# Cross-attention and a state-space scan on one core: the denominators' products placed later, features in contiguous chunks, and a planner with longer transfer times

## The chip, the core and the metric

The kernel runs on one core of one Trainium2 chip. Its engines are TensorE (PE in the profile, its weight loads PEld), VectorE (DVE), ScalarE (ACT), GpSimd (POOL) and SyncE (SP), which here does nothing but issue DMAs. The metric is the device time of one execution in microseconds (us). All data is float32.

## The reference

With T = 4096 rows of x, 3202 rows of context, a width H = 512, 8 heads of 64 and a state of 64, the reference computes (batch 1):

```python
xq  = layernorm(x, g1, beta1);  kv = layernorm(ctx, g1, beta1)
q, k, v = xq @ Wq.T + bq, kv @ Wk.T + bk, kv @ Wv.T + bv      # 8 heads of 64
x1  = x + softmax(q k.T / 8) v @ Wo.T + bo                     # over all 3202 keys
u   = (layernorm(x1, g2, beta2) @ W_in.T + b_in) @ Bmat        # [4096, 64]
s_t = silu(s_{t-1} @ A.T) + u_t                                # scan over 4096 steps
out = x1 + s @ Cmat + mean(ctxb) @ W_prog.T + b_prog
```

The token ids have no part in the output.

## The kernel before

**Stages.** For the first 215 us or so the kernel normalizes the context in 26 chunks of 128 rows, turns each (TensorE transposes, L285), and makes keys (pk) and values (pv), which it stores in DRAM in the layout in which they will be read. Small pieces of work (biases, the folded weight of the state's input, the first queries) are threaded between the chunks (`side`). Then comes the attention, and from about 1945 us on the end of the scan and the output.

**Attention.** The queries are cut into 8 blocks Q of 512 rows, each into 4 pairs of heads hp and 2 halves of 256 rows: 64 units. A unit goes through the keys in 13 steps of up to 256 keys. In a step, TensorE makes the scores s (L649: 16 matmul instructions of 64x64 by 64x256, four of which lie beside each other in the array), ACT takes their exponential p (L719), VectorE, or GpSimd at steps 2, 6 and 10, adds p to the unit's running sum acc (L727), and four steps later TensorE multiplies p with the values into po (L759). A maximum over sampled keys (sm, L667 and L686) gives the shift of the exponent. At the end of a unit the sum is folded on GpSimd (`fold`, L734), and `sums` multiplies it with ones on TensorE: pd (L777, 8 matmul instructions), the denominators. ACT reads pd (L811), VectorE adds its two parts (L815), takes the reciprocal (L818), scales the unit's output (L825) and reduces once for a check (L821).

**Around a block.** When the units of a half are done, the output projection pa multiplies with Wo (L1000), VectorE adds the residual rows (x1, L1013), which GpSimd has prepared (xr, L994), and the rows are normalized, turned and multiplied into the scan's input (pu, L1056). Queries of the next block are loaded, normalized, turned and multiplied (pq, L318). In the middle blocks (0 < Q < 7) rows are not turned by TensorE: VectorE transposes squares of 32x32 (`flip`, L946), and `move` (L951) puts the squares in their places by DMA, 16 DMAs of 32 KB for each pair of tiles, four in each of four pieces of the plan.

**Features.** The 512 features of a row lie on 128 partitions in 4 chunks. For queries and for the rows after the first sum, before has feature 4p + c in chunk c of partition p (`slice(c, None, NC)` in `transposes`), so a partition's features are contiguous in the weight's rows and a move goes in pieces of 256 floats. The weight of the queries, its gain and its bias (raw_q, g1q, be1q) and those of the second norm (g2s, be2s) are loaded in that order, the gains and biases by 16 small DMAs. The context's features are in contiguous chunks of 128.

**The order of work.** The program is written by hand for the first stage. For the rest, `Plan` (L68) orders pieces of work: each has an engine, an estimated cost in ns, a due time, pieces after which it comes, and rings of buffers that it takes and that other pieces give back. `Plan.order` runs a clock over them: an engine that is free takes the ready piece that is due first; what depends on a piece on another engine becomes ready `LATE` ns after it ends (L76; for SP this stands for the time of a transfer). A step is due every STEP = 2150 ns. The order so found is the order of instructions on each engine; on the chip engines wait for each other by semaphores, and each engine's instructions run in this order. The ring `m` has two PSUM banks, used in turn by pd (both), pa (both), pq, pu and the transposes (tp). `from_(d)` (L847) names the score step that belongs to a due time, so that a piece can be held behind it. K and V tiles are loaded 10 and 6 steps ahead, from the same SP queue as moves, rows (xr) and queries (x).

The pieces that the change touches are `sums` in `finish` (L800) and the `move` pieces in `queries` (L882) and `project` (L978):

```python
plan.add(("sums", i), "PE", 450, partial(sums, w), [("fold", i)], d + 1000,
         ["s"] if last else ["m", "m"], [("acc", ("add", i, 1))], "quarters")
...
plan.add((*ks[0], f"move{a}"), "SP", 1300, partial(move_, a), ...
```

Here d is the time of a unit's last product, and `last` is true for the last unit alone.

In the last unit pd is called pd_last and takes a bank pair of the ring s; the products of the last half's outputs with Wo are called yb (L1347), and are in the plan as pieces ("last", c), the last of which need the last unit's scaled output.

Of the kernel before, what the change touches and what calls it, by code (L numbers as in the profile page):

```python
# [20 lines left out]
P = 128  # L21
TB = 32
# [45 lines left out]
class Plan:  # L68
# [6 lines left out]

    LATE = {"PE": 110, "DVE": 130, "ACT": 110, "POOL": 100, "SP": 3000}  # L76
    ENTER, LEAVE = 110, 147
# [93 lines left out]
def xattn_ssm_kernel(  # L171
# [50 lines left out]
    be2s = const.tile([P, NC], F32, name="be2s")  # L222
    g1q = const.tile([P, NC], F32, name="g1q")
    be1q = const.tile([P, NC], F32, name="be1q")
    bqkv = const.tile([P, 3 * NC], F32, name="bqkv")
# [78 lines left out]
    def turned(xn, xh, t, name):  # L304

        tp = transposes(None, "m", xh, P, name)
        yield
        n = 2 * TB
        nc.scalar.copy(
            xn[:, t * P // n : (t + 1) * P // n].rearrange("p a c k -> p c a k"),  # L310
            tp.rearrange("p c (a k) -> p c a k", k=n),
        )
# [21 lines left out]
    def first_queries(x0):  # L334

        xn = first_xn["xn"] = xnp.tile([P, QB // (2 * TB), NC, 2 * TB], F32, tag="xn", name="xn_0")
# [12 lines left out]
        pieces = heads(0, 0, xn)  # L349
        next(pieces)  # L350
        for _ in pieces:
            yield
        yield
# [14 lines left out]
    def fetch_w(k, queue, part=slice(0, NC)):  # L368
        of = wsrc if k else wqkv_t.rearrange("(p c) o -> p c o", c=NC)
        queue.dma_start(raw[k][:, part], of[:, part, k * H : (k + 1) * H])  # L370

    def gain(k, w):
        for i in range(NC):
            nc.vector.tensor_scalar(
                w[:, i, :], raw[k][:, i, :], (g1s if k else g1q)[:, i : i + 1], None, ALU.mult
            )
# [9 lines left out]
    def shift(k):  # L386

        t = weighted(raw[k], be1s if k else be1q, f"shift_{k}")
# [14 lines left out]
        yield  # L403


    def side():
# [43 lines left out]
        for i in range(NC):  # L450
            nc.tensor.matmul(
                pt[:, i, :NS], wct[:, i::NC], twice, start=True, stop=True
            )
# [64 lines left out]

    def turned_c(xh, n, name):
        return transposes(kps, "t", xh, n, name, lambda c: slice(c * P, (c + 1) * P))  # L520

    def turn_chunk(c):
        if c < NCH:
            g, n = c // GC, keys(c)
            if c % GC == 0:
                cts[g] = ctp.tile([P, NC, GC * CK], F32, tag="ct", name=f"ct_{g}")
            o = key0(c) - key0(g * GC)
            copy = nc.vector.tensor_copy if c % 2 else nc.scalar.copy
            copy(cts[g][:, :, o : o + n], turned_c(xhs.pop(c), n, f"c{c}"))  # L529

    with tc.manual_schedule():
# [7 lines left out]
        load_chunk(3)  # L539
        for t, src in ((be1s, beta1), (bqkv, b_qkv)):  # L540
            nc.sync.dma_start(t, src)
        for c in range(4, 7):
            load_chunk(c)
        for t, src in ((g1q, g1), (be1q, beta1), (g2s, g2), (be2s, beta2)):
            for k in range(NC):
                n = P // NC
                nc.sync.dma_start(t[k * n : (k + 1) * n], src.rearrange("(p c) k -> k p c", c=NC)[k])
        norm_chunk(0)
# [251 lines left out]
    def finish(w, i, d, plan):  # L800
# [22 lines left out]
        def scale(part):  # L823
# [58 lines left out]
    def queries(plan, Q, d):  # L882
# [3 lines left out]
        for half in range(2):  # L886
# [17 lines left out]
            def open_(half=half):  # L904
                if half == 0:
                    w["xn"] = xnp.tile([P, QB // (2 * TB), NC, 2 * TB], F32, tag="xn", name=f"xn_{Q}")

            def move_(a, half=half, v=v, open_=open_):
                if a == 0:
                    open_()  # L910
                move(w["xn"][:, half * P // TB : (half + 1) * P // TB], v["x"], a)

            def turn(half=half, nv=nv, at=at, v=v, open_=open_):
                open_()
                xn = w["xn"][:, half * P // TB : (half + 1) * P // TB]
# [6 lines left out]
            if mixes(Q):  # L922
# [21 lines left out]
    def flip(pair, xh, t):  # L944

        nc.vector.transpose(  # L946
            pair.rearrange("p t h -> p (t h)").rearrange("p (b c t r) -> p t b c r", b=P // TB, c=NC, t=2)[:, t],
            xh.rearrange("p (b r c) -> p b c r", b=P // TB, c=NC),
        )

    def move(xn, pair, a):  # L951

        of = pair[a * TB : (a + 1) * TB].rearrange("p t h -> p (t h)").rearrange(
            "p (b c k) -> p b c k", b=P // TB, c=NC
        )
        for b in range(P // TB):
            nc.sync.dma_start(xn[b * TB : (b + 1) * TB, a], of[:, b])

# [19 lines left out]
    def project(plan, Q, halves, d, index):  # L978

        for half in halves:  # L980
# [71 lines left out]
            def inputs(w=w, at=at, last=last):  # L1052
                w["pu"] = m_tile([P, P], f"pu_{at[0]}")
                for c in range(NC):
                    for t in range(2):
                        nc.tensor.matmul(  # L1056
                            w["pu"][t * NS : (t + 1) * NS], wc[:, c, :],
                            w["xn"][:, t, c, :] if last else w["xn"][:, :, c, t * TB : (t + 1) * TB],
                            start=(c == 0), stop=(c == NC - 1), skip_group_check=True,
                        )  # L1060
# [20 lines left out]
            else:  # L1081
                copied, xn2, after = [], (*ks[0], "move0"), 16

                def move_(a, w=w, at=at):
                    if a == 0:
                        w["xn"] = xp_.tile([P, P // TB, NC, 2 * TB], F32, tag="xn2", name=f"xn2_{at[0]}", bufs=1)
                    move(w["xn"], w["x1"], a)
# [5 lines left out]
                for a in range(P // TB):  # L1093
                    plan.add((*ks[0], f"move{a}"), "SP", 1300, partial(move_, a),
                             [(*k, "flip") for k in ks] + ([xn2] if a else []), d + (6 + 2 * a) * STEP,
# [256 lines left out]
    def last_rows(plan, d):  # L1352
# [26 lines left out]
        def turn_(g):  # L1379
            if g:  # L1380
                tp = v["tp"][g] = sv["pyl"].rearrange("p (c k) -> p c k", c=NC)
                for c in range(NC):
                    nc.tensor.transpose(tp[:, c, :], v["xh"][g][:, c::NC], ident)
            else:
# [269 lines left out]
    def attend():  # L1654
# [31 lines left out]
        def turned_():  # L1686
# [6 lines left out]
            for c in range(NC):  # L1693
                nc.tensor.transpose(banks[0][:, c * P : (c + 1) * P], xh[:, c::NC], ident)
            nc.scalar.copy(xn, banks[0].rearrange("p (c k) -> p c k", c=NC))
# [204 lines left out]
```

## Time and profile before

| | us |
|---|---|
| median of 3 runs | 2019.77 |
| lowest and highest | 2015.93, 2020.21 |
| the profiled execution | 2018.0 |
| its span, first to last instruction | 2016.0 |
| TensorE busy | 1965.9 (98%) |
| VectorE busy | 1277.6 (63%) |
| ScalarE busy | 1131.9 (56%) |
| GpSimd busy | 791.7 (39%) |
| DMA queue of SP, share of 16 engines | 32.5% |
| granted TensorE clock, mean | 0.991 |

The profile is of one execution. A group is named by its line, engine and operation and by the tiles that it writes and reads (out<-in). Matmul instructions are pipelined: one is counted as busy until its modelled end, so groups overlap in the list, and the starts tell the rate at which they issue. Lines of the view in order of time have start, length, engine, line, operation, tiles, shape and count, and in brackets the idle time of the engine before it and what ended it. Lines of the view of waits have the waiting group, what ended the wait, and the total in us, the times and the longest. Lines of the table by stretches have the stretch, its length, the busy us (and instructions) of PE, PEld, DVE, ACT and POOL, the granted TensorE clock as a share of full speed, the DMA engines' share and GB/s.

### The profile page before, as it was taken

The page shows a single profiled execution, that of the slowest core. Times are in us where ns is not written, and L with a number is a line of the kernel's source. Part 1 is how long each engine was busy: PE and PEld are TensorE (multiplying, and loading weights), DVE is VectorE, ACT ScalarE, POOL GpSimd, SP SyncE. Part 2 cuts the span into 40 slices and gives each one's busy share as a digit, 9 for nine tenths or more (in the row PEclk, how much of TensorE's full clock was granted, in tenths as well). Part 3 has the DMA queues.
Part 4 walks back from the last instruction along what each step waited for, and adds up shares of the span by engine and source line. Part 5 has one row for each costly group of instructions (what it writes and reads, how often), then busy time and mean ns, then how long its engine had stood idle before and what let it go on. Part 6 is the DMA issues. An engine that isn't in the chain of part 4 may idle for free.

```text
span 2016.0 us, 66547 instructions
## 1 busy us (share of the span) xinstructions
PE 1965.9 (98%) x29070; PEld 1261.4 (63%) x29070; DVE 1277.6 (63%) x1533; ACT 1131.9 (56%) x1478; POOL 791.7 (39%) x631
## 2 busy tenths in 40 slices
PE   8999999999999999999999999999999999999996
PEld 4444566666566666666666666666666666666774
DVE  4221367566866687567856686668756665666585
ACT  2233466565556556655656656655665665655653
POOL 2111244344533444345424443344434552444424
PEclk9999999999999999999999999999999999999998
DMA  5632323223322233223322332223312321445476
GB/s 170 190 99 66 102 82 98 65 81 104 103 76 78 88 102 98 61 74 98 96 62 80 105 103 77 78 86 103 98 57 78 98 75 59 139 132 154 135 200 200
DMA packets 209014, 204.29 MB, mean 101 GB/s; under 512 B 29576, under 2 KB 182152, under 8 KB 208716
## 3 DMA queue, kind: packets, MB, share of 16 engines
q1 hardware_dynamic: 204168, 192.28, 32.5%
q10 hardware_dynamic: 4548, 7.67, 1.2%
q8 instruction: 231, 3.78, 0.8%
q14 instruction: 67, 0.55, 0.1%
HBM read 156.33 MB, written 29.88 MB: 92 GB/s over the span
## 4 chain that ended last, share of the span: by engine, by line
PE 91%; DVE 3%; POOL 2%; issue 1%; DMA 1%; ACT 1%; SPq 0%; DVEq 0%; ACTq 0%; POOLq 0%
PE po L759 33%; PE s L649 33%; PE pq L318 6%; PE pa L1000 5%; PE pk L598 4%; PE pv L565 4%; PE pd L777 2%; DVE acc L727 1%; PE pu L1056 1%; PE sm L667 1%; PE po L747 1%; ACT p L719 1%; POOL acc L734 1%; PE tp_c L285 1%; DMA xr<-in_x_dram 0%
## 5 line engine op out<-in xcount | busy, mean ns | idle before, releaser
L719 ACT ACTIVATE p<-s,shifts 128x1024 f32<-128x1024 f32 (+1 forms) x832 | 886.7, 1080 | 557.5 <-PE s L649 539.8
L649 PE MATMUL s<-q,k 64*64 64x256 f32 x12800 | 841.1, 379 | 3.5 <-ACT p L719 2.5
L759 PE MATMUL po<-p,v 64*64 64x256 f32 x12800 | 834.1, 378 | 0.4 <-DVE o L798 0.4
L727 DVE TENSOR_TENSOR acc<-p,acc 128x1024 f32<-128x1024 f32 (+1 forms) x515 | 625.4, 1214 | 319.1 <-POOL acc L727 270.2
L727 POOL TENSOR_TENSOR acc<-p,acc 128x1024 f32<-128x1024 f32 x189 | 460.7, 2437 | 706.0 <-DVE acc L727 380.0
L649 PEld LDWEIGHTS s<-q,k 64*64 64x64 f32 x12800 | 490.9, 133 | 229.2 <-ACT p L719 24.6
L759 PEld LDWEIGHTS po<-p,v 64*64 64x64 f32 x12800 | 494.5, 134 | 198.4 <-issue 12.3
L734 POOL TENSOR_TENSOR acc<-acc 128x512 f32<-128x512 f32 x64 | 89.7, 1401 | 116.4 <-DVE acc L727 114.2
L727 DVE TENSOR_TENSOR acc<-p,p 128x1024 f32<-128x1024 f32 x64 | 100.6, 1572 | 48.4 <-ACT p L719 42.8
L318 PE MATMUL pq<-xn,wq 128*128 128x512 f32 x256 | 118.3, 605 | 0.0
L818 DVE RECIPROCAL rd<-rd 128x256 f32<-128x256 f32 (+1 forms) x65 | 112.3, 1728 | 2.2
L1000 PE MATMUL pa<-wo,o 128*128 128x512 f32 x240 | 107.0, 599 | 0.0
L713 DVE TENSOR_TENSOR acc<-x,acc 2x256 f32<-2x256 f32 x128 | 97.6, 762 | 2.9
L565 PE MATMUL pv<-wv,ct 128*128 128x512 f32 (+1 forms) x208 | 96.3, 616 | 1.0 <-ACT ct L529 0.7
L598 PE MATMUL pk<-ct,wk 128*128 128x512 f32 (+1 forms) x224 | 88.8, 549 | 0.0
L318 PEld LDWEIGHTS pq<-xn,wq 128*128 128x128 f32 x256 | 46.0, 189 | 57.6 <-issue 56.3
L1000 PEld LDWEIGHTS pa<-wo,o 128*128 128x128 f32 x240 | 44.4, 190 | 56.0 <-issue 55.8
L327 ACT ACTIVATE q<-pq,bias 128x512 f32<-128x512 f32 x32 | 22.0, 687 | 98.6 <-PE pq L318 98.6
L529 DVE COPY ct<-tp_c 128x512 f32<-128x512 f32 (+1 forms) x13 | 8.5, 651 | 105.7 <-PE tp_c L285 105.7
L798 DVE TENSOR_TENSOR o<-po,o 128x256 f32<-128x256 f32 x64 | 27.0, 421 | 71.2 <-ACT o L794 70.8
L994 POOL TENSOR_TENSOR xr<-xr,rowb 128x512 f32<-128x512 f32 x30 | 45.9, 1544 | 57.6 <-DMA xr<-in_x_dram 57.6
L565 PEld LDWEIGHTS pv<-wv,ct 128*128 128x128 f32 (+1 forms) x208 | 38.3, 193 | 44.8 <-issue 42.6
(215 smaller groups left out, 1221.2 us busy)
## 6 DMA issues: line engine op xcount, KB each, us to landing
k<-kd SPq DMA_DIRECT2D x432, 128.0 KB, 2.2
v<-vd SPq DMA_DIRECT2D x432, 128.0 KB, 2.2
xn<-x SPq DMA_DIRECT2D x416, 32.0 KB, 1.9
xr<-in_x_dram SPq DMA_DIRECT2D x30, 256.0 KB, 3.7
x1d<-xr SPq DMA_DIRECT2D x30, 256.0 KB, 2.7
x<-in_x_dram SPq DMA_DIRECT2D x28, 256.0 KB, 3.5
cx<-in_ctx_dram SPq DMA_DIRECT2D x25, 256.0 KB, 3.2
vd<-vs SPq DMA_DIRECT2D x25, 256.0 KB, 2.2
```

The costliest lines, as they stand in the source:

```text
L318: nc.tensor.matmul(pq, wq[:, i, hp * P : (hp + 1) * P], xn[:, :, i, :], start=(i == 0), stop=(i == NC - 1),)
L565: nc.tensor.matmul(pv[h * HD : h * HD + n, :H], ct[:, k, o : o + n], wv[:, k, :], start=(i == 0), stop=(i == NC // parts - 1), skip_group_ ...
L598: nc.tensor.matmul(pk[:, :n_g], wk[:, i, hp * P : (hp + 1) * P], ct[:, i, :n_g], start=(i == 0), stop=(i == NC - 1),)
L649: nc.tensor.matmul(s[k0 : k0 + HD, a, b, :], kts[(*w["at"][:2], c)][r, b * CK + k0 : b * CK + k0 + HD], q[r], start=True, stop=True, skip_ ...
L713: nc.vector.tensor_tensor(to[r], t[r], to[r], ALU.add)
L719: nc.scalar.activation(t[:, :, :nb, :], w["ps"][c][:, :, :nb, :], AF.Exp, bias=w["shift"])
L727: engine.tensor_tensor(w["acc"][:, :, :nb, :], t[:, :, :nb, :], before[:, :, :nb, :], ALU.add)
L734: nc.gpsimd.tensor_tensor(acc[:, :, 0, :], acc[:, :, 0, :], acc[:, :, 1, :], ALU.add)
L759: nc.tensor.matmul(w["po"][a * HD : (a + 1) * HD, k, :QU], vts[Q, hp, c][r, b, a * HD : (a + 1) * HD], t[r, a, b, :], start=(c == 0 and b ...
L818: nc.vector.reciprocal(w["rd"][:, part], w["rd"][:, part])
L994: nc.gpsimd.tensor_tensor(v["x"], v["x"], rowb, ALU.add)
L1000: nc.tensor.matmul(v["pa"], o_t[Q, c, half][:, t * P : (t + 1) * P], wo[:, c, :], start=(c == 0), stop=(c == NC - 1),)
```

## The change

There are four parts.

1. `sums` of all units but the last is held behind the score step that is due six steps after the unit's last product.
2. Queries and rows have their features in contiguous chunks of 128 like the context: `transposes` takes columns c*128 to (c+1)*128, `xn` is [128, 4, rows] instead of [128, rows/64, 4, 64], the query weight is read like the others, and the separate gains and biases (g1q, be1q) and the 16 small loads go; g2s and be2s come by one DMA each. `flip` reads its squares contiguously.
3. `move` issues as many DMAs of the same size, each in pieces of 64 floats (256 bytes) instead of 256 floats.
4. In the plan a piece of four moves costs 2600 instead of 1300, and `LATE` of SP is 5000 instead of 3000.

```diff
-    LATE = {"PE": 110, "DVE": 130, "ACT": 110, "POOL": 100, "SP": 3000}
+    LATE = {"PE": 110, "DVE": 130, "ACT": 110, "POOL": 100, "SP": 5000}
...
-    def transposes(pool, tag, xh, n, name, of=lambda c: slice(c, None, NC)):
+    def transposes(pool, tag, xh, n, name):
...
-                tp[:, c, :n], xh[:n, of(c)], ident[:n, :n]
+                tp[:, c, :n], xh[:n, c * P : (c + 1) * P], ident[:n, :n]
...
-                xn[:, :, i, :],
+                xn[:, i, :],
...
-        of = wsrc if k else wqkv_t.rearrange("(p c) o -> p c o", c=NC)
-        queue.dma_start(raw[k][:, part], of[:, part, k * H : (k + 1) * H])
+        queue.dma_start(raw[k][:, part], wsrc[:, part, k * H : (k + 1) * H])
...
-        for t, src in ((be1s, beta1), (bqkv, b_qkv)):
+        for t, src in ((be1s, beta1), (bqkv, b_qkv), (g2s, g2), (be2s, beta2)):
             nc.sync.dma_start(t, src)
         for c in range(4, 7):
             load_chunk(c)
-        for t, src in ((g1q, g1), (be1q, beta1), (g2s, g2), (be2s, beta2)):
-            for k in range(NC):
-                n = P // NC
-                nc.sync.dma_start(t[k * n : (k + 1) * n], src.rearrange("(p c) k -> k p c", c=NC)[k])
...
-        plan.add(("sums", i), "PE", 450, partial(sums, w), [("fold", i)], d + 1000,
+        plan.add(("sums", i), "PE", 450, partial(sums, w),
+                 [("fold", i)] + ([] if last else [from_(d + 6 * STEP)]), d + 1000,
                  ["s"] if last else ["m", "m"], [("acc", ("add", i, 1))], "quarters")
...
-                    plan.add((*ks[0], f"move{a}"), "SP", 1300, partial(move_, a),
+                    plan.add((*ks[0], f"move{a}"), "SP", 2600, partial(move_, a),
...
     def flip(pair, xh, t):
 
         nc.vector.transpose(
-            pair.rearrange("p t h -> p (t h)").rearrange("p (b c t r) -> p t b c r", b=P // TB, c=NC, t=2)[:, t],
-            xh.rearrange("p (b r c) -> p b c r", b=P // TB, c=NC),
+            pair.rearrange("p t h -> p (t h)").rearrange("p (g t r) -> p t g r", t=2, r=TB)[:, t],
+            xh.rearrange("p (g r) -> p g r", r=TB),
         )
 
     def move(xn, pair, a):
 
+        n = 2 * TB
         of = pair[a * TB : (a + 1) * TB].rearrange("p t h -> p (t h)").rearrange(
-            "p (b c k) -> p b c k", b=P // TB, c=NC
+            "p (c b k) -> p b c k", b=P // TB, k=n
         )
         for b in range(P // TB):
-            nc.sync.dma_start(xn[b * TB : (b + 1) * TB, a], of[:, b])
+            nc.sync.dma_start(xn[b * TB : (b + 1) * TB, :, a * n : (a + 1) * n], of[:, b])
...
-                            w["xn"][:, t, c, :] if last else w["xn"][:, :, c, t * TB : (t + 1) * TB],
+                            w["xn"][:, t, c, :] if last else mixed(w["xn"][:, c, :], t),
```

The same change of columns and shapes is made in `turned`, `first_queries`, `side`, `open_`, the rows of the last half and the slow path that runs only if a check of the softmax or the scan fails.

More of the change, by code (lines that the diff above doesn't have):

```diff
@@ L222, in xattn_ssm_kernel @@
     be2s = const.tile([P, NC], F32, name="be2s")
-    g1q = const.tile([P, NC], F32, name="g1q")
-    be1q = const.tile([P, NC], F32, name="be1q")
     bqkv = const.tile([P, 3 * NC], F32, name="bqkv")
@@ L307, in turned @@
         yield
[L308 to L312, printed above, removed]
+        nc.scalar.copy(xn[:, :, t * P : (t + 1) * P], tp)
     def heads(Q, hp, xn):
@@ L334, in first_queries @@
     def first_queries(x0):
-        xn = first_xn["xn"] = xnp.tile([P, QB // (2 * TB), NC, 2 * TB], F32, tag="xn", name="xn_0")
+        xn = first_xn["xn"] = xnp.tile([P, NC, QB], F32, tag="xn", name="xn_0")
         for t in range(NT):
@@ L374, in gain @@
             nc.vector.tensor_scalar(
-                w[:, i, :], raw[k][:, i, :], (g1s if k else g1q)[:, i : i + 1], None, ALU.mult
+                w[:, i, :], raw[k][:, i, :], g1s[:, i : i + 1], None, ALU.mult
             )
@@ L386, in shift @@
     def shift(k):
-        t = weighted(raw[k], be1s if k else be1q, f"shift_{k}")
+        t = weighted(raw[k], be1s, f"shift_{k}")
         yield
@@ L451, in side @@
             nc.tensor.matmul(
-                pt[:, i, :NS], wct[:, i::NC], twice, start=True, stop=True
+                pt[:, i, :NS], wct[:, i * P : (i + 1) * P], twice, start=True, stop=True
             )
@@ L517, in norm_chunk @@
             xhs[c] = normalize(cxs.pop(c), keys(c), f"c{c}", pool=cin)
-    def turned_c(xh, n, name):
-        return transposes(kps, "t", xh, n, name, lambda c: slice(c * P, (c + 1) * P))
     def turn_chunk(c):
@@ L528, in turn_chunk @@
             copy = nc.vector.tensor_copy if c % 2 else nc.scalar.copy
-            copy(cts[g][:, :, o : o + n], turned_c(xhs.pop(c), n, f"c{c}"))
+            copy(cts[g][:, :, o : o + n], transposes(kps, "t", xhs.pop(c), n, f"c{c}"))
     with tc.manual_schedule():
@@ L905, in open_ @@
                 if half == 0:
-                    w["xn"] = xnp.tile([P, QB // (2 * TB), NC, 2 * TB], F32, tag="xn", name=f"xn_{Q}")
+                    w["xn"] = xnp.tile([P, NC, QB], F32, tag="xn", name=f"xn_{Q}")
             def move_(a, half=half, v=v, open_=open_):
@@ L910, in move_ @@
                     open_()
-                move(w["xn"][:, half * P // TB : (half + 1) * P // TB], v["x"], a)
+                move(w["xn"][:, :, half * QU : (half + 1) * QU], v["x"], a)
             def turn(half=half, nv=nv, at=at, v=v, open_=open_):
                 open_()
-                xn = w["xn"][:, half * P // TB : (half + 1) * P // TB]
+                xn = w["xn"][:, :, half * QU : (half + 1) * QU]
                 v["turns"] = [turned(xn, nv[t]["xh"], t, f"x{at[t]}") for t in range(2)]
@@ L1085, in move_ @@
                     if a == 0:
-                        w["xn"] = xp_.tile([P, P // TB, NC, 2 * TB], F32, tag="xn2", name=f"xn2_{at[0]}", bufs=1)
+                        w["xn"] = xp_.tile([P, NC, QU], F32, tag="xn2", name=f"xn2_{at[0]}", bufs=1)
                     move(w["xn"], w["x1"], a)
@@ L1093, in project @@
                 for a in range(P // TB):
-                    plan.add((*ks[0], f"move{a}"), "SP", 1300, partial(move_, a),
+                    plan.add((*ks[0], f"move{a}"), "SP", 2600, partial(move_, a),
                              [(*k, "flip") for k in ks] + ([xn2] if a else []), d + (6 + 2 * a) * STEP,
@@ L1382, in turn_ @@
                 for c in range(NC):
-                    nc.tensor.transpose(tp[:, c, :], v["xh"][g][:, c::NC], ident)
+                    nc.tensor.transpose(tp[:, c, :], v["xh"][g][:, c * P : (c + 1) * P], ident)
             else:
@@ L1693, in turned_ @@
             for c in range(NC):
-                nc.tensor.transpose(banks[0][:, c * P : (c + 1) * P], xh[:, c::NC], ident)
+                cs = slice(c * P, (c + 1) * P)
+                nc.tensor.transpose(banks[0][:, cs], xh[:, cs], ident)
             nc.scalar.copy(xn, banks[0].rearrange("p (c k) -> p c k", c=NC))
```

## The prediction

> **What bounds the kernel now.** I read the page first, then the waits, then the products of the denominators (pd, L777), then TensorE in order of time at each place where pd stood late.
>
> ```profile
> PE 1965.9 (98%) x29070; PEld 1261.4 (63%) x29070; DVE 1277.6 (63%) x1533; ACT 1131.9 (56%) x1478; POOL 791.7 (39%) x631
> PE 91%; DVE 3%; POOL 2%; issue 1%; DMA 1%; ACT 1%; SPq 0%; DVEq 0%; ACTq 0%; POOLq 0%
> ```
>
> TensorE (PE) is the chain. The change adds no matmul and takes none away, so time can only come from TensorE's stops. Who causes them between 215 and 1945 us:
>
> ```profile
> PE pd L777 <- DVE x L1013: 10.2, 10, 1.8
> PE pd L777 <- POOL acc L734: 6.1, 7, 3.0
> PE s L649 <- ACT p L719: 2.5, 6, 0.4
> PE s L649 <- DMA k<-kd: 1.0, 1, 1.0
> ```
>
> Nearly all of it stands before pd: it waits for the fold of its sums (POOL L734), or for the two PSUM banks that the output projection (pa) used until VectorE added x1 (L1013). In order of time, one block Q (218.4 us) shows both:
>
> ```profile
> 702.58 1.04 PE L649 MATMUL s<-q,k 64*64 64x256 f32 x16
> 704.28 0.66 PE L777 MATMUL pd<-acc,ones 64*64 64x256 f32 x8 [0.65 <-POOL acc L734]
> ...
> 735.84 1.04 PE L649 MATMUL s<-q,k 64*64 64x256 f32 x16
> 737.80 0.61 PE L777 MATMUL pd<-acc,ones 64*64 64x256 f32 x2 [0.91 <-DVE x L1013]
> 739.22 0.44 PE L777 MATMUL pd<-acc,ones 64*64 64x256 f32 x3 [0.81 <-DVE x L1013]
> ```
>
> A group of 16 issues in 0.864 us (next starts show it), so the first pd could start at 703.45 and starts at 704.28: 0.83 late. The second could start at 736.70 and is 1.09 late; its second bank comes at 739.22, so that its last matmul starts 1.71 after its first instead of 0.24, which costs 1.47 more. What follows is a slow stretch:
>
> ```profile
> 736.70:740.10 3.40, 1.67 (x22) 0.85 (x22) 3.26 (x7) 1.29 (x2) 2.05 (x3) 1.00 0.76 252
> 740.10:743.50 3.40, 3.40 (x37) 2.14 (x32) 2.63 (x4) 1.12 (x5) 3.12 (x6) 0.50 0.25 71
> ```
>
> In the 3.4 us of the stop TensorE was busy for 1.67; in the next 3.4 us its granted clock (the column after POOL) is 0.50, which costs 3.4 x 0.5 = 1.7 us of work. Such a stretch stands at 521.7, 740.1, 958.6, 1177.0 and 1395.5 us, each behind such a stop.
>
> Why x1 is late there and not at the first projection of the block:
>
> ```profile
> 686.97 0.69 DVE L1013 TENSOR_TENSOR x<-pa,xr 128x512 f32<-128x512 f32 x1 [0.83 <-PE pa L1000]
> ...
> 715.12 2.52 POOL L994 TENSOR_TENSOR xr<-xr,rowb 128x512 f32<-128x512 f32 x2 [8.10 <-DMA xr<-in_x_dram]
> 717.60 2.37 POOL L727 TENSOR_TENSOR acc<-p,acc 128x1024 f32<-128x1024 f32 x1
> ```
>
> At the first projection VectorE is waiting for pa and ends x1 0.73 us after it (687.66 against 686.93). At the second, POOL sat 8.10 us behind a load of xr with an add queued after it; VectorE's adds of that unit follow late, and x1 stands in VectorE's queue behind them (last x1 end 739.17, pa end 734.13).
>
> **The change, part by part.** *(1) pd six steps on.* In the built order the typical pd moves from behind score step 4 of the next unit to behind step 9. The two that stop move by 6.8 us of TensorE work (fold case) and 5.6 us (x1 case). They were up to 0.83 late for the fold and 2.5 to 3.4 for x1, so both are covered with 2 us or more to spare. What it takes away, from the starts at each place:
> - fold, six blocks: 0.65, 0.83, 0.66, 0.66, 0.67, 0.67, and 0.05 each for the refilled pipeline: 4.4 us;
> - x1, first bank, five blocks: 1.95, 1.09, 1.09, 1.81, 1.04: 7.0 us;
> - x1, second bank: 5 x 1.47 = 7.4 us;
> - the late fold at 1604.83: 3.2 us, and one of 0.2 at 324;
> - five stretches at half clock: 5 x 1.7 = 8.5 us.
>
> Together 30.7 us. The page's waits give less (16.3) because a matmul counts as busy beyond its issue slot.
>
> What is late next: pd now follows the *first* projection by 2.69 us of work. By the row above x1 is done 0.73 after pa, so some 1.7 us are spare; I take 0, bound 0 to 5.1 per block (the worst of the second). ACT reads pd right after the exp of step 9, with as many instructions as before. scale comes five steps later; the first projection of a block needs units that ended 13 steps before it, the second stands 24 steps further on: 0. With no stops for ACT to catch up in, waits of s for p may grow: the longest now is 0.6 us, so 6 blocks x 0.3 to 0.6; I take +2.
>
> *The end.* Now pd_last starts at 1954.54, and the denominators' chain (ACT, sum, reciprocal, scale) ends at 1958.0, while six yb products of 0.86 us each hide it. In the new order four of them (3.4 us) stand ahead of pd_last and two behind: the chain of 3.5 us is covered for 1.7 + 0.4 only, so +1.3. The unit before now finishes (0.42 + 1.75 + 0.43 + 0.41 = 3.0 us of VectorE) nearer to the last adds; the fold, at 1954.49, may come at 1957.5, still before pd_last's new place. I take +1.2, bound 0 to 4.
>
> *Last block, first half.* The small products pu follow their transposes by 1.72 us of work instead of 3.44; two ACT copies of 0.59 behind an exp of 1.11 need 2.3: +0.6, bound 0 to 1.2.
>
> *(2) Layout.* Transposes of strided columns start 120 ns apart, those of contiguous ones 109: 44 of them on tiles of x and y become contiguous, 44 x 11 ns = -0.5. pq and pa issue at 429 ns with and without strides: 0. The flips (52 of 1.12 to 1.14 us) read with stride now; contiguous, they cost between 0.69 (statistics of the same size) and 1.14. VectorE, 68% busy in the loop, hides that: 0, a gain of VectorE time alone.
>
> *(3) Moves.* 416 DMAs keep their 32 KB but go from 32 pieces of 1 KB to 128 of 256 B. In the packets, 1 KB took 46 ns (median), 512 B 27, 256 B 18 (on ACT's queue, from HBM). So 1.5 to 2.3 us of engine time a move, times 416 over 16 engines: +21 us for each engine, 1% of the span. The issue:
>
> ```profile
> 708.91 2.40 SPq L957 DMA_DIRECT2D xn<-x  x4
> 23.38 0.38 SPq L579 DMA_DIRECT2D vd<-vs  x1
> 14.97 2.53 SPq L547 DMA_DIRECT2D be1q<-in_L_xattn_beta_dram  x4
> ```
>
> A move is issued in 0.60 us; vd with 512 pieces in 0.38, be1q with 128 pieces in 0.63. So -0.2 to +0.03 each; I take 0, by the last, which has the same 32 x 4 shape. pq stands seven steps (15 us) behind the last move, pu more, k and v loads are six to ten steps ahead: 0 on the path. The Trainium skill speaks against this part: "DMA: Bandwidth & Descriptors", Specifications, wants pieces of at least 512 B, since smaller ones are read, modified and written. By that a 256 B piece would cost no less than one of 512 B, an estimate of 128 x 27 ns = 3.5 us a move, still beside the path; the 18 ns do not show it, but no move of 256 B stands in this trace.
>
> *(4) The plan.* 2600 for four moves fits the 2.4 us measured better than 1300, so POOL's order now has the add before the xr rows that blocked it 8.10 us: this supports (1), counted at 0.
>
> *(5) Setup.* 16 tiny loads (10.2 us of SP) go. TensorE waited there for VectorE (1.2 and 1.5 us before pb) and for nothing they delay: 0, bound -1.
>
> Sum: 2018.0 (this execution; span 2016.0) - 30.7 + 2 + 1.2 + 0.6 - 0.5 = 1990.6. The median of the runs is 1.8 above this execution; I say 1992.
>
> **Rivals.**
> - *Half speed stays, or a third of the stops do.* If the slow stretches have a cause of their own, their 8.5 us remain: 2000. Against: each stands right behind a stop, and none elsewhere between 215 and 1945. If VectorE's queue still makes x1 late in places, 10 us remain: 2002. The case holds 1998 to 2012, with 0.15. The Trainium skill bears on its first half: "TensorE: Matmul & The Clock Gate", Part 1, has the clock fall after an idle window of about 3.4 us. By that a stop of 1 to 2.5 us would not do it; the row, 1.7 us idle of 3.4 before the fall, speaks for the stops.
> - *The stops move to another wait.* VectorE is 68% busy in the loop (1178 of 1730 us); if it falls behind, buffers of p come late, ACT waits for them and s for ACT. Against: ACT's waits on POOL and VectorE before p sum to 7 us now. About 2018: 0.07.
> - *Slower: x1 behind the first projection.* pd waits there as it does now behind the second, in seven blocks (Q 1 to 7). The 1.7 us spare and the clock's 1.7 cancel, so x1 ending L us later costs 7 L. The gain without it is 27.4: it breaks even at L = 3.9 us and makes the kernel slower by 4 us at 4.5. At the worst stop seen (3.4 + 1.7) it costs 36: 2028. Against: the 0.73, and less work ahead of x1 in VectorE's new order. 0.08.
> - *Slower: issue grows with the pieces.* Four times 0.60 would put xr, behind 16 moves, 29 us later; pa, now 9.5 us behind the end of its rows (727.07 against 717.60), would stop for some 20 us in six blocks: 2110. It decides where the stop and the clock's 1.7 reach (27.4 + 4) / 6 = 5.2 us a block: xr 13 us later, 1.4 us a move. Against: vd's 0.38. 0.04.
>
> **Numbers.** The forecast, 1984 to 1998, has 0.66. Two runs tell apart about 0.2% (4 us). Faster: 0.66 + 0.15 and a little of the others, 0.82; same 0.06; slower 0.12. The range takes in the second case: 1984 to 2012.
>
> **What would show it.** Idle before pd near zero and the wait for L1013 gone; no half clock between 215 and 1945; blocks of 213 instead of 218.4 us; a short stop before the last yb; moves at about 0.6 us to issue. It is wrong if pd still waits behind the first projection, if xr lands later against pa, or if s waits for p by more than 10 us in all.

## The result and the profile after

The kernel after takes 2005.5 us (median of 5), the kernel before 2017.7 beside it: a ratio of 0.9941 with a 95% interval of 0.9926 to 0.9956. The forecast was 1992: the sign was right, less than half of the size came (12 us instead of 26 to 27). The profiled execution takes 2004.45 us with a span of 2002.6 (before 2016.0).

Who stops TensorE between 215 and 1945 us in the kernel after (engine, line and tile waiting, releaser: us in all, times, longest):

```profile
PE po L745 <- DVE o L784: 10.6, 8, 2.6
PE s L635 <- ACT p L705: 3.9, 10, 0.4
PE pu L1044 <- DMA xn<-x: 1.1, 1, 1.1
PE s L635 <- issue: 1.0, 1, 1.0
PE yb L1335 <- DVE o L811: 1.0, 1, 1.0
```

No line with pd is left. In its place stands a wait that the kernel before hardly had: the first product of a unit (po, L745) waits for join (L784, VectorE adds half of po to the other half, which ScalarE has copied out), which reads the one PSUM bank that po takes. From the start times, ten such stops cost 12.4 us of TensorE's issue (before: one, 0.6). The worst, 2.81 us at 328 us, has the half clock behind it, the only slow stretch left in the loop. The columns are the window, its length, busy time (instructions) of PE, PEld, DVE, ACT and POOL, the granted clock, the DMA share and GB/s:

```profile
325.30:328.70 3.40, 0.77 (x16) 0.51 (x16) 3.40 (x3) 2.40 (x3) 2.77 (x2) 1.00 0.00 0
328.70:332.10 3.40, 3.40 (x44) 2.17 (x38) 3.30 (x4) 0.00 (x0) 0.33 (x1) 0.54 0.02 5
```

One of the ten in order of time, on four engines (start, duration, engine, line; in brackets idle time and releaser):

```profile
754.81 1.09 PE L635 MATMUL s<-q,k 64*64 64x256 f32 x16
757.04 1.96 PE L745 MATMUL po<-p,v 64*64 64x256 f32 x32 [1.13 <-DVE o L784]
...
743.65 1.75 DVE L804 RECIPROCAL rd<-rd 128x256 f32<-128x256 f32 x1
...
748.91 2.45 DVE L713 TENSOR_TENSOR acc<-p,acc 128x1024 f32<-128x1024 f32 x2
752.20 1.25 DVE L713 TENSOR_TENSOR acc<-p,p 128x1024 f32<-128x1024 f32 x1 [0.84 <-ACT p L705]
753.48 3.05 DVE L699 TENSOR_TENSOR acc<-x,acc 2x256 f32<-2x256 f32 x2
756.56 0.42 DVE L784 TENSOR_TENSOR o<-po,o 128x256 f32<-128x256 f32 x1
...
753.46 2.37 POOL L713 TENSOR_TENSOR acc<-p,acc 128x1024 f32<-128x1024 f32 x1
...
754.65 0.37 ACT L780 COPY o<-po 128x256 f32<-128x256 f32 x1
```

ScalarE's copy ends at 755.02, and join could start then. It starts at 756.56, because rest (L699, the two small adds of the remaining keys) stands ahead of it on VectorE and takes 3.05 us, where the same two instructions alone take 0.84 (at 322.82 us of the same trace): POOL's add runs from 753.46 to 755.83 beside them. The Trainium skill ("SBUF — State Buffer", Who interferes with whom) describes this: a VectorE instruction with both inputs in SBUF shuts out, or is shut out by, a GpSimd instruction that reads SBUF. The row agrees: the first half of rest takes 2.62 us instead of 0.42 and ends 0.27 after POOL's add.

The later products come in further up. The finish of the denominators (sum, reciprocal, scale and reduction on VectorE, 743.20 to 746.19) now stands ahead of two of the unit's last adds, which end at 751.36; POOL's add of step 10 comes behind them, and behind the norm's small instructions on POOL, and so runs beside rest. In the run below that has all of the change but the later products, that POOL add starts at 746.16, before rest (751.75), and po does not wait. VectorE itself had caught up in the kernel after (it is idle for 0.84 us before 752.20), so at this place join is late because of where POOL's add has come to lie, and not because VectorE is full.

The rows of the second projection on POOL, which before waited 8.10 us with an add queued behind them, now stand behind that add:

```profile
709.50 2.39 POOL L713 TENSOR_TENSOR acc<-p,acc 128x1024 f32<-128x1024 f32 x1 [4.06 <-DVE acc L713]
714.60 4.25 POOL L982 TENSOR_TENSOR xr<-xr,rowb 128x512 f32<-128x512 f32 x2 [2.72 <-DMA xr<-in_x_dram]
```

### The profile page after: what moved, and what is told of

It reads as the page before. It is cut to its first block, busy times and chain, and to the rows that moved or that the text cites. A ratio compares the mean times of both kernels' runs of the same rounds, so it can differ in the third digit from the quotient of the medians.

```text
span 2002.6 us, 66617 instructions
## 1 busy us (share of the span) xinstructions
PE 1954.1 (98%) x29070; PEld 1251.4 (62%) x29070; DVE 1259.4 (63%) x1533; ACT 1130.1 (56%) x1478; POOL 789.5 (39%) x631
## 5 line engine op out<-in xcount | busy, mean ns | idle before, releaser
L745 PE MATMUL po<-p,v 64*64 64x256 f32 x12800 | 822.6, 377 | 10.6 <-DVE o L784 10.6
L635 PE MATMUL s<-q,k 64*64 64x256 f32 x12800 | 826.5, 377 | 4.9 <-ACT p L705 3.9
L713 DVE TENSOR_TENSOR acc<-p,acc 128x1024 f32<-128x1024 f32 (+1 forms) x515 | 633.3, 1230 | 249.0 <-POOL acc L713 179.4
L713 POOL TENSOR_TENSOR acc<-p,acc 128x1024 f32<-128x1024 f32 x189 | 449.2, 2376 | 679.1 <-ACT p L705 362.2
L635 PEld LDWEIGHTS s<-q,k 64*64 64x64 f32 x12800 | 482.6, 133 | 233.3 <-ACT p L705 32.5
L745 PEld LDWEIGHTS po<-p,v 64*64 64x64 f32 x12800 | 487.8, 133 | 209.7 <-DVE o L784 15.2
L699 DVE TENSOR_TENSOR acc<-x,acc 2x256 f32<-2x256 f32 x128 | 95.2, 744 | 2.5
L784 DVE TENSOR_TENSOR o<-po,o 128x256 f32<-128x256 f32 x64 | 27.1, 423 | 84.3 <-ACT o L780 83.7
L584 PEld LDWEIGHTS pk<-ct,wk 128*128 128x128 f32 x224 | 39.2, 190 | 42.6 <-issue 42.6
```

The lines of the kernel that those rows point to most:

```text
L584: nc.tensor.matmul(pk[:, :n_g], wk[:, i, hp * P : (hp + 1) * P], ct[:, i, :n_g], start=(i == 0), stop=(i == NC - 1),)
L635: nc.tensor.matmul(s[k0 : k0 + HD, a, b, :], kts[(*w["at"][:2], c)][r, b * CK + k0 : b * CK + k0 + HD], q[r], start=True, stop=True, skip_ ...
L699: nc.vector.tensor_tensor(to[r], t[r], to[r], ALU.add)
L713: engine.tensor_tensor(w["acc"][:, :, :nb, :], t[:, :, :nb, :], before[:, :, :nb, :], ALU.add)
L745: nc.tensor.matmul(w["po"][a * HD : (a + 1) * HD, k, :QU], vts[Q, hp, c][r, b, a * HD : (a + 1) * HD], t[r, a, b, :], start=(c == 0 and b ...
L784: nc.vector.tensor_tensor(o, rows_of(w, w["po"][:, 1, :QU], True), o, ALU.add)
```

## The experiments

The change has three parts that can be tried apart: the later **products** of the denominators, the **layout** (contiguous chunks and flips, 256-byte moves, setup) and the plan's two **numbers**. All ratios are against the kernel before on the same chip, from 4 or more runs of each kernel.

### The parts, first round

*The products alone:* in the kernel before, `[("fold", i)]` of sums becomes

```
[("fold", i)] + ([] if last else [from_(d + 6 * STEP)])
```

> The kernel before with nothing changed but the place of the denominators' products (six score steps on). Theory 1 (the place sets everything: the stops before pd go, and the finish of the denominators, now at the end of the unit on VectorE, makes join late, so that the first product of a unit waits for its one PSUM bank): VectorE's order is that of the kernel after, so the time is that of the kernel after within 2 us, 2003 to 2008, with some 12 us of waits before po. Theory 2 (the small pieces of the moves and the new layout cost what the forecast missed): they are not in it, so it comes near the forecast, 1990 to 1996, without waits before po. Theory 3 (the plan's new costs of the moves do part of the work, since they put an add of POOL ahead of the rows it waits 8 us for): waits of pd for x1 remain, 2008 to 2015.

Measured: 2026.8 us, ratio 1.0033 (1.0020 to 1.0045), slower than before.

*Layout and numbers without the products:* the kernel after with that edit taken back.

> The kernel after with the denominators' products at their old place: layout, moves of 256 bytes and the plan's numbers alone. Theory 1: the time of the kernel before within 3 us, 2014 to 2021, all stops before pd there again (16 us of waits before pd). Theory 2: slower than before by up to the 15 us that the forecast missed, 2022 to 2033, with waits for xn or xr. Theory 3: faster than before, 2005 to 2012, since x1 is no longer late.

Measured: 2007.1 us, ratio 0.9936 (0.9922 to 0.9949), the same as the kernel after. So the first theory falls, and with it the forecast's main term: the part that was to bring 30.7 us brings nothing here and costs 7 us alone. The waits of the run with the products alone, and then of the run without them:

```profile
PE po L759 <- DVE o L798: 19.2, 8, 4.0
PE s L649 <- ACT p L719: 3.9, 10, 0.4
PE pa L1001 <- DVE rd L815: 1.9, 1, 1.9
```

```profile
PE sm L672 <- DVE m L665: 4.4, 5, 0.9
PE s L635 <- ACT p L705: 3.1, 8, 0.4
PE pd L763 <- DVE x L1000: 3.0, 5, 0.6
PE pu L1043 <- DMA xn<-x: 2.8, 2, 1.6
```

In the first the stops of pd for x1 and the late fold are gone as forecast, but po's stops for join cost 20.8 us of issue. Half clock takes 13.6 us (before: 8.5): 11.9 of it at these stops, 1.7 behind a new one, where the projection (pa, third line), whose banks pd had used, waits until VectorE has added pd's parts. In the second the half clock and all fold waits but one (0.75 us) are gone although pd stands at its old place; of x1 only the second bank's waits remain, a little shorter (1.23 instead of 1.47 us a block), and spread, the small product that hands on a unit's sampled maximum, newly waits for it (sm, 5.3 us).

### Join and the distance

*Rest behind join:* the kernel after with one dependency more.

```
 plan.add(("rest", i), "DVE", 1200, partial(rest, w),
-         [("add", i, 1), ("extra", first)],
+         [("add", i, 1), ("extra", first)] + ([("join", i - 1)] if i else []),
```

> The kernel after, with one dependency more: the add of the remaining keys (rest) of a unit stands behind join of the unit before it on VectorE. Theory 1: join runs as soon as ScalarE has copied its half, the waits of po for join (10.6 + 15.2 us in the two views, 12.4 us in TensorE's issue) and the half clock behind the one at 328 go: 1990 to 1995. Rival (VectorE is too full in those units, and the stop only moves on): rest is later by join's wait, POOL's add behind it too, buffers of p come late, and the time stays at 2002 to 2008 with waits elsewhere.

Measured: 1999.9 us, ratio 0.9903 (0.9888 to 0.9919). po's stops fall from 12.4 to 3.2 us of issue, but pu now waits 5.1 us, for moves and a load of v, and the stop before yb costs 3.05 instead of 1.1, with 1.7 us of half clock behind it. The stop of po is what was said; half of it is handed on, and the time misses the 1990 to 1995.

*Four steps instead of six:* `from_(d + 4 * STEP)`.

> The kernel after with the denominators' products four score steps on instead of six. Theory 1 (the finish's 3.0 us of VectorE are too near the unit's end): VectorE does them some 4 us earlier, adds 8 and 9 stand ahead of the end again, join is on time at most units, and pd is still covered for about two steps (4.3 us) against stops that were 0.8 to 3.4 us: 1992 to 1999, waits before po under 4 us. Rival (join is late for another reason, POOL's adds that stretch VectorE's): waits before po stay near 12 us, 2003 to 2008. Rival (x1 still stands in the way): waits of pd for x1 come back, 2005 to 2012.

Measured: 2008.6 us, ratio 0.9937 (0.9924 to 0.9951), as with six. The finish's place does set po's stops (0.2 us left in the view of waits), but s waits for p in 24 places (12.6 us of issue) and pu in eight (9 us). The miss is in the time: the stop moved on once more.

### The numbers, the layout and one exchange on POOL

*The numbers alone:* the kernel before with `"SP": 5000` in `LATE` and 2600 for a piece of four moves.

> The kernel before with nothing changed but the plan's two numbers (transfers land 5000 instead of 3000 ns behind their issue, four moves cost 2600 instead of 1300). The run without the later products kept the whole gain, so the first theory fell. Theory A (the numbers do it: on POOL the add of step 6 now stands ahead of the rows of the second projection, which wait 8 us for their load, so VectorE's adds, join and x1 behind it are early): 2004 to 2010, no wait of pd for the fold, x1 about 2 us behind pa instead of 3.4. Theory B (the layout does it: the flips take 0.68 instead of 1.14 us and VectorE has 0.9 us less in front of each adds' chain): 2015 to 2021, stops as before.

Measured: 2014.2 us, ratio 0.9970 (0.9957 to 0.9982), half of what theory A said; the waits for the fold, which it had going, stay.

*The layout alone:* the run without the products, with the two old numbers.

> The kernel before with the layout alone: features in chunks of 128, contiguous flips, moves in pieces of 256 bytes, setup without the small loads; products of the denominators and the plan's numbers as before. Theory A: 2015 to 2021, the POOL rows still wait some 8 us with an add behind them, and the stops before pd are there. Theory B: 2004 to 2010. If the small pieces cost something that the plan's numbers hide: over 2022.

Measured: 2018.7 us, ratio 0.9988 (0.9977 to 1.0000). Waits of pd stay (12.0 us for x1).

*One exchange on POOL:* the kernel before, where the rows of the second projection come behind the add.

```
 plan.add((*ks[t], "row"), "POOL", 1300, partial(row, vs[t]),
-         [(*ks[t], "load")], d - STEP)
+         [(*ks[t], "load")] + ([("add", int(d / STEP) // NDC, 6)] if half and not last else []), d - STEP)
```

> The kernel before with one dependency more in the plan: the rows of the second projection of a block stand behind POOL's add of step 6 of the unit that runs then. The layout, the numbers and the order on SP stay; on POOL two instructions change places in six blocks. Theory A: this one exchange brings most of the gain, 2005 to 2012, x1 some 2 us behind pa and no fold wait above 0.3 us. If the numbers act in another way (the order of loads and moves on SP, other engines' orders): 2015 to 2021. Theory B: 2015 to 2021.

Measured: 2007.4 us, ratio 0.9941 (0.9925 to 0.9957): two instructions of POOL in another order in six blocks, and the time is that of the whole change. POOL at the second projection, against the rows of before in the prediction:

```profile
712.58 2.38 POOL L727 TENSOR_TENSOR acc<-p,acc 128x1024 f32<-128x1024 f32 x1 [7.48 <-DVE acc L727]
714.90 3.49 POOL L994 TENSOR_TENSOR xr<-xr,rowb 128x512 f32<-128x512 f32 x2
```

The add starts at 712.58 instead of 717.60; 1.9 us of this is that TensorE is ahead there, so it is 3.1 us earlier against the score steps. The rows pay little: they start at 714.90, as their load has just landed, and end at 718.39 (before: 717.64), well ahead of pa (725.07). VectorE's adds follow POOL's: the first x1 there starts 2.3 us after the start of the last pa matmul instead of 3.4 (733.90 - 731.61 against 736.97 - 733.54), the late fold of 3.2 us is gone, and of the half clock 1.7 us remain of 8.5. Not all of theory A came: fold stops of 0.64 to 0.82 us stay in six blocks (it said none above 0.3), the second bank still costs some 1.4 us in five, and spread newly waits 5.3 us for its maximum (the line with sm below is the same in this run).

The numbers alone set the same exchange, but they also put the moves later in SP's order, and pu waits for them (first line below):

```profile
PE pu L1056 <- DMA xn<-x: 5.2, 5, 1.4
PE sm L686 <- DVE m L679: 4.4, 5, 0.9
PE pd L777 <- DVE x L1013: 4.1, 5, 0.8
PE s L649 <- ACT p L719: 3.1, 8, 0.4
PE pd L777 <- POOL acc L734: 2.8, 6, 0.5
```

*The kernel after with the old numbers:*

> The kernel after with the plan's two old numbers: later products and new layout stay. Theory A: as the run with the later products alone, slower than before: 2022 to 2030, with 15 to 21 us of waits of po for join, since POOL's add stands behind the rows again and the finish of the denominators comes on top. Theory B: as after, 2003 to 2009.

Measured: 2017.2 us, ratio 0.9986 (0.9974 to 0.9998). Without the exchange the gain is gone, as theory A said; the 2022 to 2030 was too high, since with the layout po's stops are half as long (10.4 instead of 20.8 us). As with the products alone, one projection waits for the banks that pd took: pa starts 4.3 us late at 1854.50, right after VectorE's sum of pd's parts (1854.03 to 1854.45).

### What the layout brings, and the last corner

*Products and numbers without the layout:*

> The kernel before with the later products and the plan's numbers, without the layout. Runs so far put the exchange on POOL first (1.0 with it alone: all of the gain) and the layout second. If the layout's share comes from the flips (each 0.45 us longer here, eight of them in a block on VectorE ahead of adds and join), the po stops of the kernel after grow by some 0.4 to 0.9 us each and the waits of pu for the moves by 1 to 2 us: 2009 to 2017. If the layout brings nothing where the products come late: 2003 to 2008, as the kernel after.

Measured: 2008.0 us, ratio 0.9934 (0.9921 to 0.9948): with the new numbers, where the products come late, the layout brings nothing. With the old numbers it does bring something beside the late products (1.0033 alone, 0.9986 with the layout).

*Longer flips:* layout and numbers, with the second half of each flip done a second time.

```
+ nc.vector.transpose(<the same out>[:, t, NC * 2 :], <the same in>[:, NC * 2 :])
```

> The layout and the plan's numbers with the products at their old place, and the second half of each flip done a second time, so that a flip takes about 1.05 us again as it did with strides; the moves stay in pieces of 256 bytes. If VectorE's time in the flips is what the layout gave over the plan's numbers alone (2014 without, 2007 with it): 2010 to 2015, waits of pd for the fold back at 3 to 4 us. If the pieces or another part of the layout gave it: 2004 to 2008.

Measured: 2017.1 us, ratio 0.9981 (0.9970 to 0.9991), against 0.9936 without the second half. In the groups, a flip is now 0.69 + 0.45 = 1.13 us (mean in ns at the end of the columns before the idle time), as with strides (1.12 to 1.14):

```profile
L932 DVE STREAM_TRANSPOSE x<-xh_y 128x512 f32<-128x512 f32 x28 | 19.2, 685 | 34.1 <-POOL acc L713 29.0 <-ACT xh_y L857 5.1
L936 DVE STREAM_TRANSPOSE x<-xh_y 128x256 f32<-128x256 f32 x28 | 12.5, 446 | 1.0
```

The waits of pd for the fold are back too, 3.6 us (said 3 to 4). So 0.45 us in each of 52 flips, 23 us of an engine that is busy for 63% of the span, are worth some 9 us of the end. The time is even 3 us above the numbers alone (2014), hardly more than the intervals allow, with 7.9 instead of 5.2 us of waits of pu for moves; whether the 256-byte pieces or the two-part flip cause that was not separated.

The eight corners, ratio to the kernel before:

| | old numbers | new numbers |
|---|---|---|
| neither | 1 | 0.9970 |
| products | 1.0033 | 0.9934 |
| layout | 0.9988 | 0.9936 |
| both | 0.9986 | 0.9941 |

The new numbers set the exchange on POOL. With it, products or layout bring another 0.35%, and the second of them brings nothing. With the old numbers no corner gains more than 0.14%.

### Building on it

*Layout and exchange, old numbers:*

> The layout and the exchange on POOL (rows of the second projection behind the add of step 6), with the plan's old numbers and the products at their old place. The exchange alone gave 2007 with 5.0 us of fold waits and 5.6 us at the second bank; the shorter flips should take 4 us of the first and 1 us of the second, and the waits of pu for the moves (5 to 6 us with the new numbers) should stay away: 2000 to 2005. If the numbers do something else that is needed: 2007 to 2012.

Measured: 2001.4 us, ratio 0.9905 (0.9889 to 0.9920): pu's waits for moves are gone, as expected; the shorter flips take 2.9 us from the fold stops and 0.8 us from the second bank (said 4 and 1). This beats the kernel after.

*Layout, exchange, products, rest behind join, old numbers:*

> The layout, the exchange on POOL, the later products and rest behind join, with the plan's old numbers. The version with join first and the new numbers took 1999.9, with 5 us of waits of pu for the moves, which should go with the old numbers, 3.2 us of po for join and 3 us of yb: 1993 to 1998. If the moves were not what the numbers delayed: 1998 to 2002, with the waits of pu still there.

Measured: 1996.4 us, ratio 0.9875 (0.9860 to 0.9890).

*The same without the products:*

> The best version so far (layout, exchange on POOL, rest behind join, old numbers; 1996.4) with the products of the denominators back at their old place. If the later products are worth something once join no longer stands behind the finish: the stops at pd's second bank (4.6 us) and of spread for its maximum (5.3 us) come back and it takes 2001 to 2007. If they only exchange one wait for another: 1994 to 1999.

Measured: 2008.7 us, ratio 0.9952 (0.9939 to 0.9966), but it does not answer: one stop of 8.7 us in the last block, with 5.1 us of half clock behind it, is most of it. POOL there:

```profile
1837.22 1.26 POOL L981 TENSOR_TENSOR xr<-xr,rowb 128x512 f32<-128x512 f32 x1 [15.15 <-issue]
1838.44 2.35 POOL L713 TENSOR_TENSOR acc<-p,acc 128x1024 f32<-128x1024 f32 x1
```

It is the same trap as at the second projection: POOL idle for 15 us at rows (the profile names no releaser), an add behind them.

*POOL's add of step 10 behind join* (the kernel after). The condition takes in seven units: the one with the stop of 2.81 us, the five with 1.2 to 1.3 us, and one with 0.2 us; two stops of 1.3 and 1.5 us, at 1587 and 1836 us, lie elsewhere:

```
+ ([("join", i)] if c == 10 and i % 8 == 3 and Q < NQB - 1 else [])
```

> The kernel after; in the plan POOL's add of step 10 stands behind join in the six units whose end had the po stops of 1.2 to 1.5 us, so that it no longer runs beside rest; VectorE keeps rest ahead of join. If join was late because rest took 3.05 us beside POOL's add instead of 0.84: rest takes 0.84, those po stops fall from 7.9 us in all to under 1 us, and the time to 1996 to 2000 (or the later add costs some of that back at the fold: to 2003). If join was late only because of what stands ahead of it in VectorE's order: rest is short but po still waits over 0.8 us there, 2003 to 2008.

Measured: 2006.7 us, ratio 0.9948 (0.9934 to 0.9961), no change. At the place itself it does what was said (VectorE):

```profile
752.06 0.84 DVE L699 TENSOR_TENSOR acc<-x,acc 2x256 f32<-2x256 f32 x2
753.63 0.42 DVE L784 TENSOR_TENSOR o<-po,o 128x256 f32<-128x256 f32 x1 [0.73 <-ACT o L780]
...
775.60 2.90 DVE L699 TENSOR_TENSOR acc<-x,acc 2x256 f32<-2x256 f32 x2
778.53 3.98 DVE L713 TENSOR_TENSOR acc<-p,acc 128x1024 f32<-128x1024 f32 x2
782.44 0.41 DVE L784 TENSOR_TENSOR o<-po,o 128x256 f32<-128x256 f32 x1
```

Rest takes 0.84 and join no longer waits for it. But the work that was put off stands ahead of the next unit's join, which starts 5.5 us after ScalarE's copy, with a stop of 1.5 us; in six blocks the stop has moved one unit on. So the collision with POOL sets where po stops. That the load of the two engines around these units sets that it stops at all fits, and is not shown.

*The exchange in the last block too*, with the products and without them (`if half or last` in the edit of the exchange):

> The best version (layout, exchange, later products, rest behind join, old numbers: 1996.4) with the same exchange in the last block too, where POOL stands at the rows, behind a load, from 1824 to 1837 us with the add of step 6 behind them; nothing else changes place on any engine. If an add behind rows that wait is what costs: the stop of 3.6 us of s for p at 1852 and the half clock around it (3.4 us) go, 1989 to 1994. If it is the load that is late: the projection of that block waits instead, 1995 to 1999.

> The same without the later products (the run before this one had a stop of 8.7 us in the last block, again at the rows of POOL, and 5.1 us of half clock behind it, that hid the answer). If the later products are worth something in this version: po stops of 7 us remain here, 1996 to 2001, and the other run is faster by 5 us or more. If they are worth nothing: within 3 us of the other.

Measured: with the products 1994.8 us, ratio 0.9864 (0.9847 to 0.9880); without 1996.7, ratio 0.9876 (0.9859 to 0.9892). The stop at 1852 and its half clock are gone, but with the products two stretches at half clock, 6.8 us long each, now lie at the stops before yb and in the scan (1929.5 and 1939.8 us). That the time fell by only 1.6 us is therefore not evidence against the exchange. Between the two, 1.9 us, less than can be told apart, and it has that half clock in it: the later products are worth some 0.1% in the best version, with intervals that leave room for nothing and for 0.3%. Without them po stops for 7.0 us (five times 1.4), as expected, with them for 2.8; what they take away there comes back at other places.

## Why the prediction was right and wrong

**The step that failed** is in part (1): "What is late next", with "scale comes five steps later ... : 0". It asked who waits for scale, and found the projections far away. It did not ask what the finish (sum, reciprocal, scale and reduction, 3.0 us of VectorE) is put ahead of. At its new place it stands before two of the last adds of the unit; POOL's add behind them comes to lie beside rest, and behind rest stands join, which frees po's one bank. I counted those 3.0 us only at the end of the program. The term of 0 measured 12.4 us of stops and 1.7 of half clock in the kernel after, and 20.8 and 11.9 with the products alone. Put in place of 0, those 14.1 us make the prediction's sum 2004.7, and the profiled execution took 2004.45; the smaller terms were not each checked, so that it is as close as this is luck. It is shown that the place does it in this version: without the later products, and with them four steps on instead of six, the stops of po are all but gone. It is not the only thing that can: with rest behind join they are there without the later products too.

**The second step** that failed is part (4), "counted at 0". Its observation was right (the add now stands before the rows that blocked it 8.10 us), and it had even been named as the reason why x1 is late. But I took it as support of (1), where it takes away the same stops at their source: alone it makes the kernel 12 us faster (0.59%): the first bank's waits (7.0 us), the late fold (3.2) and 6.8 us of half clock go, and the spread's new wait (5.3) takes part of that back. The sum counted the stops as belonging to the part that could cover them, without asking whether another part removes them.

**The third** is in part (2): flips of VectorE time "0" because the engine is 68% busy in the loop. The duration came out at its lower bound (0.68 to 0.69), and with the exchange in place the layout brought 0.34% (0.9936 against 0.9970) and 0.36% (0.9905 against 0.9941).

**Right:** the stops of pd for the fold and x1 went, with the half clock behind them; s for p grew by some 2.4 us (said +2); the stop before the last yb is 1.1 us (said 1.2). A move issues in 0.60 us (median; before 0.59) and lands after 1.9 as before. The packets of 256 B took 20 ns (median; said 18), 2.6 us of engine time a move. The rule of the Trainium skill ("DMA: Bandwidth & Descriptors", Specifications) would have made it 3.5, an estimate; no run here isolates what the pieces cost. Blocks take 214.7 us (said 213).

Of the rivals, "the stops move to another wait" was the one that came in part, with the wrong wait: I had bounded it by ScalarE's waits for buffers of p and did not look at the ring with one buffer. The measured time also lies in the range of the first rival (1998 to 2012), but by luck: neither of its two conditions came, for the half clock of the loop went down to 1.7 us and no wait of pd was left.

## What to carry to other kernels

Before a stop is priced as the gain of an edit, ask which other edit removes its cause, and try each part alone: here two parts aimed at the same stops, and their gains do not add. A piece of work that is moved away from a wait is moved in front of something: list what stands behind it in its engine's new order, down to whoever frees a ring of one buffer. An instruction that waits for a load in an in-order queue should stand behind the work that is ready; that exchange of two instructions was worth as much here as the whole change.

## What the runs showed of the hardware

The half clock follows stops less regularly than I took it. In the loop, no single stop up to 1.75 us had it, 2.03 and 2.13 us had it in two kernels, but 2.13, 2.31 and 3.05 us passed without it in three others, and so did the late fold of 3.2 us at 1604.8 us in the kernel before itself, which the prediction had not set against its rule. The Trainium skill ("TensorE: Matmul & The Clock Gate", Part 1) speaks of a free-running window of about 3.4 us; that would fit such a spread by phase, and no run here varies the phase by itself. What the traces add is that stops of 2 to 3 us, shorter than the window, can be enough. A VectorE add of two SBUF operands beside a POOL add took up to 3.3 us instead of 1.2 (at 319.50 us in the kernel after), so that 3 us in a queue is not a fixed amount of time.
